# The first expert block's 512 rows prepared in the planned first pass, in the output weights' storage; a bias scaled on ScalarE; new due times

## The chip, the cores and the metric

The kernel runs on one core of a Trainium2 chip. The metric is the device time of one execution in microseconds (us), the median of three runs. A run takes in both layers of the network from the inputs in device memory to the output there; no work is done on the host.

## The reference

The input `x` has 64 graphs of 256 nodes with 256 features, and `adj` is a 0/1 matrix for each graph, stored as int32. Two layers follow one another, each of a graph part and a feed-forward part, and each part adds its result to `x`:

```python
x = x + gat(layernorm(x), adj, W, a)            # softmax over neighbours, 256x256 a graph
x = x + mamba2(layernorm(x), W_in, conv_w, ..., W_out, W_lin, b_lin)   # one chunk of 256, 8 heads of 64
x = x + rgcn(layernorm(x), adj, weight, bias)   # relation ids 1..4; adj holds 0 and 1 here
x = x + moe(layernorm(x), gate_w, gate_b, w1, b1, w2, b2)

# moe: T = 16384 tokens, E = 8 experts, capacity C = ceil(1.25 * T / E) = 2560
idx = argmax(softmax(x @ gate_w + gate_b)); prb = that probability
hmid = relu(buf @ w1[e] + b1[e])                # 256 -> 1024, for the tokens of expert e
y = (hmid @ w2[e] + b2[e]) * prb                # 1024 -> 256, 0 for tokens over the capacity
y = nan_to_num(y, nan=0, posinf=1e4, neginf=-1e4)
```

## The kernel before

The kernel has two passes. **Pass 1** (`first_pass`, line 482) takes the 64 graphs in 32 groups of two. A group is 512 rows, held as four tiles of 128 rows by 256 columns. For each group it runs attention (`attention`), the Mamba block (`scan`, `mix`), the relation part (`relate`), and for every second group the choice of an expert for 1024 tokens (`choose`). `choose` writes for every token a record of four numbers (token number, probability, minus the mean, inverse deviation) into a table `slots` in device memory, at the place that the token has with its expert; this is an indirect DMA on GpSimd, line 1436. The rows themselves go to `x3d` and to the output, line 1361.

Pass 1 isn't run in the order of the code. Every operation is a step (`Plan.step`) with an engine, an assumed duration, what it reads and writes, and a rank. `Plan.record` then issues all steps in an order of its own: of all engines it takes the one whose next step can begin first by the assumed durations, and among steps of one engine that could begin within 0.05 us of each other it takes the one with the smaller rank. The rank is `PACE * g + due`, with `g` the group and `due` an entry of one of two tables: `DUE` has 278 entries, one for each step of a group, and `LATE` has one for each step outside the groups. The order so found is fixed in the program, and each engine then runs its instructions in that order and waits for what each of them needs. Entries 0 and 1 of `DUE` belong to the loads of `x` and `adj` (lines 932 and 935, SyncE's queue), entry 29 to the load of `s2` (line 979), and entries 108 to 111 to the four loads of `spread` (line 1145), from which ScalarE makes the decays (line 1158).

Three **first blocks** (`first_block`, line 1443) are steps of the plan too. Each takes 512 tokens of one expert from the first 28 groups, and serves as filler at the end of pass 1. Their second product is line 1543; each of its four row tiles goes through DVE line 1549, ScalarE line 1551, five DVE instructions (lines 464 to 468, which replace what isn't finite), a DVE addition (line 1557) and an indirect DMA into the output on GpSimd (`sent`, line 477). Their results lie in four buffers `y`, two to a row tile.

The **lead block** is the first block of pass 2. The plan prepares half of it (`lead`, line 840): SyncE fetches its 512 records (line 849), DVE makes indices of them (lines 449 and 450), GpSimd gathers row tiles 0 and 1 from `x3d` into `lead_xg` (line 453), DVE normalises them (line 459), TensorE turns them (line 473), and ScalarE copies the result back over `lead_xg` (line 865).

**Pass 2** (`second_pass`, line 1624) goes through the rest of the tokens, first in whole blocks of 512 and then in quarter blocks of 128, one expert to a block. It is written in program order. Before its first block it issues weights (lines 1672 to 1682), records (line 1662), and gathers of rows: four for block 0 (row tiles 2 and 3 first, then 0 and 1; the raw rows are added to the result at the end), four for block 1, one each for quarter blocks 0 and 1. DVE normalises block 0's row tiles 2 and 3 (`rest`) and then the rows of quarter block 0 (`ahead`). A block (`experts`, line 1714) does this:

- it gathers the rows of the block after the next, and normalises those of the next (`xn`);
- first product: for each of 8 slices of 128 hidden columns two matmuls (line 1732) into a PSUM bank, then ReLU with the first bias on ScalarE (line 1737). Each matmul of the code is two matmul instructions in the profile. Block 0 does this in two halves of 256 rows, with the turning of row tiles 2 and 3 between them (`turned`, lines 1708 and 1711);
- second product: for each row tile 8 matmuls (line 1743), then DVE adds the second bias (line 1748), ScalarE scales by the token's probability (line 1749), and DVE lines 464 to 468 and 1756 and the indirect DMA of line 477 follow;
- after the second row tile of the four, TensorE turns the next block's `xn`, so it stops there until that is ready.

Pass 2's tiles lie where pass 1's were, and wait for these. The tile `wf` (line 507) holds the Mamba block's output weights; it belongs to pass 1 and is read by the matmuls of `mix` alone.

Of the kernel before, what the change touches and what calls it, by code (L numbers as in the profile page):

```python
# [20 lines left out]
P = 128  # L21
# [15 lines left out]
    -6331, -3161, 12771, 6388, -1140, 18799, -8820, -3915, -10864, 15954, -2744, -20439, 7528,  # L37
    -4617, -31541, -17200, 5602, -14762, -8419, -5891, -5603, -1541, -5405, -14791, -3990, 335,
    -20199, -23350, -2083, 2822, 14284, -5071, -6879, 4498, -5782, 6238, -17462, -2816, -33883,
    -20616, -6436, -3048, -8998, -9634, -9504, -22113, -20276, -11261, 1522, -9857, -1653,  # L40
    -15833, -9229, 2924, -22132, -17106, -4387, -35510, -16757, 3569, -2885, 4527, -1412, -8283,
    -15528, -3929, -11779, -11456, -7814, -6057, -12317, -10809, -5133, -8678, 9134, 13953,
    -13794, -23451, -4899, -21639, -22746, -10486, 27012, -17529, -1344, -3836, -5711, -23725,
    -14953, -12879, 3172, -5981, 1591, 15512, -17461, 534, 152, -19929, 1549, 14357, 7195,
    -3419, 29983, -11226, -18919, -14208, -27486, -16133, -19727, -32975, 18680, -3566, -464,
    -8894, -2901, -21861, 7237, -13596, -5780, 12376, 1844, -21884, 4880, -17265, -11181, 7161,
    -21630, 548, 14964, 3358, 3185, 2812, -16559, -8864, 11674, 270, 390, 1481, 9504, 2847,
    2431, 16079, 19662, -3898, 11518, 11847, 506, -17371, 20459, -5279, -20969, 31082, -3253,
    -3595, -970, 18447, 7039, -9745, -11902, -30335, 20548, -30229, -14082, 510, -2197, -25176,
    -18526, -28007, -18182, 10633, -26993, 8938, -10832, -10379, -11184, -15953, -1534, -10200,  # L50
    1179, -1228, -13286, -4161, 9055, 6753, 3161, 9529, -846, 3842, 15756, -9976, -8924, -10517,
    5604, -11994, -14390, -11511, 924, 7080, -3763, -2334, -14368, -21952, -16111, 7133, -3818,
    -13625, -16189, 4478, -3362, -831, -30811, -22197, 9169, -17068, 2289, -22646, -5638,
    -21211, -26355, 7956, -16785, -15433, 4253, -877, 2942, -11894, -10082, 5510, 8259, -10789,
    -3344, 791, -22653, 6991, -2251, -8409, -27482, -21823, -16753, 23439, -12372, -11445, 3310,
    22527, -8655, 2999, 1496, -8271, 10255, -15555, 8288, -35896, -6103, 7904, -13179, -16680,
    5249, -9828, -22280, 12222, -12498, 3441, -987, -8001, -4859, -9609, -5004, -31730, -12922,
    -9059, 5997, -13207, -32473, 21806, -6080, -32608, -5307, -9518,
]
LATE = [  # L60
    -63840, -55520, -59131, -55207, -59848, -61432, -57187, -57822, -56536, -55767, -53926,
    -58374, -60103, -65443, -56691, -53149, -62097, -52465, -58452, -56667, -62610, -54784,
    -65608, -59759, -57377, -56098, -61108, -61167, -57235, -56292, -60029, -60269, -55423,
    -63060, -63414, -59681, -63156, -58243, -64255, -56127, -56108, -57795, -60886, -59513,
    -60777, -59004, -59056, -58806, -59572, -53601, -56191, -58146, -57176, -54847, -56525,
    -55495, -53939, -56747, -58739, -49488, -50233, -60000, -54842, -49112, -48407, -55847,
    -60899, -53242, -54553, -52587, -54497, -52317, -53060, -55827, -53215, -50999, -56633,
    -59606, -52185, -51253, -56189, -53292, -51734, -50652, -43997, -50070, -49882, -48836,
    -53102, -52273, -56157, -60055, -50169, 1013, -1983, -728, -4765, -2369, -6423, -4345,
    -4325, -5261, -3579, -1796, -1630, -5149, -6851, -4608, -3725, -4488, -2136, -8245, -7748,  # L70
    -2950, -8122, 8006, 1788, 4824, -6193, 9606, 8820, 5666, -14159, 1157, -2894, 5812, 508,
    -8873, 9151, 4753, 9855, -1831, 1035, 7140, -2464, 8056, -3647, 371, 308, 3499, 8133, 4587,
    10125, 4843, -72, 332, 712, 3988, -4756, 10239, 636, -6535, -1479, -7990, -162, 6431, 11207,
    6866, 1481, 4338, 5632, 2772, 10504, 2221, -5019, -3263, 6153, 2958, 8184, 463, 3082, 3259,
    -744, 5246, -8874, 224, -2297, -2637, 9968, -5301, 6929, -3923, 12788, 1870, -5152, 7957,
    -1091, 8442, 5255, 977, 9080, 8105, 3506, 9391, 6154, -1644, -1231, 4565, -6856, 7951, 3020,
    10508, -4150, -1421, -3664, -1888, -297, 3392, 868, -3074, 7014, 1260, 2674, 3807, 3088,
    471, -7315, -17345, 4406, 4533, -7940, 10566, 9292, 5735, 7492, 2786, 1767, -4750, -535,
    -1766, 1723, -1381, 846, -1114, 6258, -3949, 4074, -1805, 1084, 6817, -3447, 6810, -3140,
    13076, 2332, 330, 8723, -3860, 7332, 9552, -3530, 12999, 10185, 1587, 11267, 5283, 2368,  # L80
    -565, 6790, -2563, 4983, 3103, 10465, -4403, -3174, -771, -6778, 1016, 4107, -1453, -2923,
    7230, 2679, -268, 4098, -352, 584, -10766, -12316, 7157, 1989, -7855, 10593, 10918, 2783,
    6000, 4603, 6058, -6544, -2195, -2667,
# [235 lines left out]
def gnn_mamba_rgcn_moe(ctx: ExitStack, tc: tile.TileContext, a: dict, out: bass.AP):  # L319
# [109 lines left out]
    lead_xg = const.tile([P, 2, D], F32, name="lead_xg")  # L429
# [40 lines left out]
    def lead_turned(ps):  # L470
        for k in range(2):
            for j in range(2):
                nc.tensor.transpose(
                    ps[:, (2 * k + j) * P : (2 * k + j + 1) * P], lead_xg[:, j, k * P : (k + 1) * P], ident)
# [7 lines left out]
    def first_pass(form, pass1):  # L482
# [24 lines left out]
        wf = wts.tile([P, NCT, DG], F32, name="wf")  # L507
# [332 lines left out]
        def lead(s, listed_, stored):  # L840

            meta_, place_, xg_ = (s.fixed(t) for t in (lead_meta, lead_place, lead_xg))
# [14 lines left out]
            for j in range(2):  # L857
                s.step(POOL, 1.1, lambda j=j: gathered(lead_xg[:, j, :], lead_place[:, 1, j : j + 1], x3d),
                       [place_, *stored], [(xg_, j)], late=2.0, move=0.3)
            for j in range(2):  # L860
                s.step(DVE, 0.33, lambda j=j: normed(lead_xg[:, j, :], lead_xg[:, j, :], lead_meta[:, j, :]),
                       [meta_], [(xg_, j)])
            ps = s.psum()
            s.step(PE, 0.45, lambda: lead_turned(ps()), [xg_], [ps])
            s.step(ACT, 0.48, lambda: nc.scalar.copy(
                lead_xg.rearrange("p j d -> p (j d)"), ps()), [ps], [xg_])
# [757 lines left out]
    def second_pass(form, pass2):  # L1624
# [6 lines left out]
        class Blocks:  # L1631
# [70 lines left out]
            def turned(self, xn, i, js=None):  # L1702

                js, dst = js or range(self.J), self.xnT[i % 2]
                for k in range(2):
                    ps = eps.tile([P, 512], F32, tag="ps", name="ps")
                    for o in range(len(js)):
# [3 lines left out]
                    nc.scalar.copy(  # L1711
                        dst[:, k, js[0] * P : (js[-1] + 1) * P], ps[:, : len(js) * P])

            def experts(self, i, rest=None):

                n = self.J * P
                meta, place, xg = self.meta[i % 3], self.place[i % 3], self.xg[i % 3]
# [157 lines left out]
```

## Time and profile before

| what | value |
|---|---|
| time, median of 3 runs | 2331.28 us (2331.22 to 2331.72) |
| the profiled execution's own time | 2330.76 us |
| its span, first to last instruction | 2328.8 us |
| busy: TensorE, DVE, ScalarE, GpSimd | 2234.8, 1759.9, 1664.4, 912.5 us |
| last instruction of the first blocks' product (line 1543) ends | 1752.3 us |
| last read of `wf` by a matmul begins | 1658.5 us |
| one whole block of pass 2 (from 1797.15 to 1825.58) | 28.43 us |
| first and second product of a whole block | 13.73 and 2 x 6.91 us |

The profiled execution's time is 1.96 us longer than its span, and lies 0.52 us under the median. A row of a timeline gives the start and the duration of an instruction or of several alike, its engine, line and operation, the tiles written and read, and in brackets how long the engine had been idle and which work ended that. PE is TensorE and PEld its loading of weights; POOL is GpSimd; SPq is SyncE's queue of DMA issues. The chain is the work that ended last, followed back step by step; it isn't proof that nothing else was as late.

### The profile page before, as it was taken

The page shows a single profiled execution, that of the slowest core. Times are in us where ns is not written, and L with a number is a line of the kernel's source. Part 1 is how long each engine was busy: PE and PEld are TensorE (multiplying, and loading weights), DVE is VectorE, ACT ScalarE, POOL GpSimd, SP SyncE. Part 2 cuts the span into 40 slices and gives each one's busy share as a digit, 9 for nine tenths or more (in the row PEclk, how much of TensorE's full clock was granted, in tenths as well). Part 3 has the DMA queues.
Part 4 walks back from the last instruction along what each step waited for, and adds up shares of the span by engine and source line. Part 5 has one row for each costly group of instructions (what it writes and reads, how often), then busy time and mean ns, then how long its engine had stood idle before and what let it go on. Part 6 is the DMA issues. An engine that isn't in the chain of part 4 may idle for free.

```text
span 2328.8 us, 34741 instructions
## 1 busy us (share of the span) xinstructions
PE 2234.8 (96%) x11111; PEld 1565.5 (67%) x11111; DVE 1759.9 (76%) x4396; ACT 1664.4 (71%) x3873; POOL 912.5 (39%) x992
## 2 busy tenths in 40 slices
PE   6999999999999999999999999999997999999986
PEld 4676766676776666766776667566676666666665
DVE  3899989999999999999998998799554333333342
ACT  3899989899999899999899988888522223332222
POOL 1233445354443445435354444523543222222221
PEclk7999999999999999999999999999998999999998
DMA  4343445444444445444453554424536333333436
GB/s 141 76 102 99 122 117 126 110 108 108 122 122 121 111 108 118 113 117 126 110 116 101 122 140 107 104 62 122 146 101 229 113 116 116 116 115 117 118 85 192
DMA packets 199928, 274.48 MB, mean 118 GB/s; under 512 B 28472, under 2 KB 165886, under 8 KB 199712
## 3 DMA queue, kind: packets, MB, share of 16 engines
q1 hardware_dynamic: 149968, 211.48, 29.3%
q0 software_dynamic: 46752, 58.65, 13.7%
q8 instruction: 94, 1.54, 0.3%
q10 hardware_dynamic: 2992, 1.81, 0.3%
q14 instruction: 122, 1.00, 0.1%
HBM read 187.43 MB, written 46.04 MB: 100 GB/s over the span
## 4 chain that ended last, share of the span: by engine, by line
PE 58%; ACT 14%; DVE 9%; POOL 6%; issue 6%; DMA 6%; SPq 0%; POOLq 0%; ACTq 0%; DVEq 0%
PE ps L871 27%; PE ps L1743 9%; PE ps L1732 9%; PE ps L1240 4%; POOL slots L1436 3%; ACT dm L1158 3%; PE ps L910 2%; PE ps L1216 2%; PE ps L1244 2%; ACT ev L998 2%; DMA x<-in_x_dram 1%; DMA xg<-x3d,lead_place 1%; ACT dm L1164 1%; DVE y L1098 1%; DVE dm L1232 1%
## 5 line engine op out<-in xcount | busy, mean ns | idle before, releaser
L871 PE MATMUL ps<-xnT,win 128*128 128x512 f32 x1152 | 539.3, 597 | 5.3 <-ACT xnT L915 4.4
L1158 ACT ACTIVATE dm<-spread,cs 128x256 f32<-128x256 f32 (+1 forms) x1024 | 379.1, 452 | 21.8 <-PE ps L1244 20.6
L1098 DVE SCALAR_TENSOR_TENSOR y<-ps,cw,y 128x510 f32<-128x510 f32 (+2 forms) x480 | 353.5, 738 | 34.5 <-ACT y L1091 31.9
L871 PEld LDWEIGHTS ps<-xnT,win 128*128 128x128 f32 x1152 | 206.9, 190 | 178.2 <-issue 157.1
L1743 PE MATMUL ps<-w,hid 128*128 128x256 f32 x1184 | 262.1, 379 | 0.0
L1732 PE MATMUL ps<-xnT,w 128*128 128x512 f32 (+2 forms) x736 | 257.0, 509 | 1.5 <-ACT xnT L1711 1.4
L871 PE MATMUL ps<-wf,gate 128*128 128x265 f32 x1024 | 251.8, 389 | 1.8 <-DVE gate L1254 1.8
L1743 PEld LDWEIGHTS ps<-w,hid 128*128 128x128 f32 x1184 | 223.2, 190 | 36.2 <-issue 7.7
L1232 DVE TENSOR_TENSOR dm<-dm,bc 128x1536 f32<-128x1536 f32 x128 | 224.0, 1750 | 3.0 <-ACT dm L1164 2.4
L871 PEld LDWEIGHTS ps<-wf,gate 128*128 128x128 f32 x1024 | 189.7, 190 | 46.5 <-issue 8.2
L1737 ACT ACTIVATE hid<-ps,b 128x512 f32<-128x512 f32 (+2 forms) x192 | 112.2, 591 | 140.4 <-PE ps L1732 134.5
L1732 PEld LDWEIGHTS ps<-xnT,w 128*128 128x128 f32 x736 | 128.9, 197 | 120.3 <-issue 110.0
L1164 ACT ACTIVATE dm<-dm 128x1536 f32<-128x1536 f32 x128 | 190.0, 1487 | 0.0
L1748 DVE TENSOR_TENSOR yv<-ps,b 128x256 f32<-128x256 f32 x74 | 31.4, 425 | 195.9 <-PE ps L1743 195.7
L1240 PE MATMUL ps<-dm,xdt 128*64 128x256 f32 x1024 | 168.7, 390 | 3.7 <-DVE xdt L1221 2.9
L1436 POOL DMA_INDIRECT slots<-meta,sl x128 | 145.3, 1136 | 59.4 <-issue 31.7
L879 POOL TENSOR_SCALAR ve<-mv 128x4 f32<-128x4 f32 x96 | 37.6, 392 | 322.3 <-DVE mv L892 217.2
L889 DVE BATCH_NORM_STATS2 st<-x 128x6 f32<-128x256 f32 x384 | 151.7, 413 | 8.4 <-DMA x<-in_x_dram 8.2
L871 PE MATMUL ps<-wx,xT 128*128 128x292 f32 x512 | 137.1, 409 | 0.0
L871 PE MATMUL ps<-wrel,hr 128*128 128x265 f32 x512 | 134.4, 392 | 0.8 <-ACT hr L1349 0.8
L871 PE MATMUL ps<-wh,eT 128*128 128x273 f32 x512 | 132.1, 402 | 1.9 <-ACT eT L1016 1.9
L1091 ACT ACTIVATE y<-ps,cb,cw 128x512 f32<-128x512 f32 x160 | 124.1, 776 | 2.1 <-PE ps L871 1.9
(310 smaller groups left out, 4727.8 us busy)
## 6 DMA issues: line engine op xcount, KB each, us to landing
spread<-sumd SPq DMA_DIRECT2D x128, 512.0 KB
w<-in_L_ffn_w_dram SPq DMA_DIRECT2D x50, 1024.0 KB
x<-blin POOLq DMA_DIRECT2D x32, 530.0 KB
x<-brel POOLq DMA_DIRECT2D x32, 530.0 KB
x<-in_x_dram SPq DMA_DIRECT2D x32, 512.0 KB
adji<-in_adj_dram SPq DMA_DIRECT2D x32, 512.0 KB
out_dram<-x SPq DMA_DIRECT2D x32, 512.0 KB
x3d<-x SPq DMA_DIRECT2D x32, 512.0 KB
```

What stands on the lines that cost most here:

```text
L871: nc.tensor.matmul(out_, lhsT=lhsT, rhs=rhs, start=(i == 0), stop=(i == len(pairs) - 1))
L889: s.step(DVE, 0.34, lambda j=j: nc.vector.bn_stats(sb()[:, j, :], src()[:, j, 0:D]), [(src, j)], [(sb, j)])
L1091: s.step(ACT, 0.66, lambda: nc.scalar.activation(y(), ps(), AF.Identity, scale=cw[:, c, 3:4], bias=cb[:, c : c + 1]), [ps, s.fixed(cw), s. ...
L1098: nc.vector.scalar_tensor_tensor(y3[:, :, d:], p3[:, :, : N - d], cw[:, c, k : k + 1], y3[:, :, d:], ALU.mult, ALU.add,)
L1158: nc.scalar.activation(dm()[:, q, bi, o : o + n], spr()[:, q, t1 - n : t1], AF.Relu, bias=cs()[:, 4 * h + j : 4 * h + j + 1], scale=-1.0,)
L1164: s.step(ACT, 1.38, lambda: nc.scalar.activation(dm(), dm(), AF.Exp, scale=-1.0), [], [dm])
L1232: s.step(DVE, 1.67, lambda dm=dm: nc.vector.tensor_mul(dm(), dm(), bc().unsqueeze(1).to_broadcast([P, 2, 2, N + P])), [bc], [dm], port=1)
L1240: nc.tensor.matmul(o, lhsT=xdt()[:, 2 * bi, h * 64 : (h + 1) * 64], rhs=dm()[:, q, bi, 0:N], start=True, stop=False,)
L1436: s.step(POOL, 1.1, lambda j=j: apart("slots", nc.gpsimd.indirect_dma_start(out=slots, out_offset=bass.IndirectOffsetOnAxis(ap=sl()[:, j : ...
L1732: nc.tensor.matmul(ps[:, :m], lhsT=w1[:, k, f * P : (f + 1) * P], rhs=lead_xg[:, k, :] if rest is not None and not o else xnT[:, k, o : o ...
L1737: nc.scalar.activation(hid[:, f, o : o + m], ps[:, :m], AF.Relu, bias=self.b1[i % 2][:, f : f + 1])
L1743: nc.tensor.matmul(ps[:, :D], lhsT=hid[:, f, j * P : (j + 1) * P], rhs=w2[:, f, :], start=(f == 0), stop=(f == NFT - 1),)
```

## The change

Four things are changed.

1. `lead` makes all four row tiles ready. It gathers four instead of two, normalises four, and turns them into two PSUM banks, one for each half of the features, copied by two ScalarE instructions. `lead_xg` is no tile of its own any more: it is a view of `wf`, and `wf` now lies with the constants, so that it lives through pass 2.
2. Block 0 of pass 2 does its first product at once for 512 rows, from the lead's tile. The `rest` normalisation and the turning in the middle are gone; the gathers of raw rows stay, in one loop. Its own turned tile `xnT` for even blocks moves to another pool.
3. In `experts` ScalarE scales the second bias by the probability (`bp`, an instruction ahead of the second product's matmuls in the code), and DVE does product times probability plus `bp` in one instruction. Before, DVE added and ScalarE scaled after it.
4. All entries of `DUE` and `LATE` are new; `LATE` has six more, for the lead's six more steps.

```diff
 DUE = [
-    -6331, -3161, 12771, 6388, -1140, 18799, -8820, -3915, -10864, 15954, -2744, -20439, 7528,
...
-    -20199, -23350, -2083, 2822, 14284, -5071, -6879, 4498, -5782, 6238, -17462, -2816, -33883,
...
-    -3419, 29983, -11226, -18919, -14208, -27486, -16133, -19727, -32975, 18680, -3566, -464,
...
+    -26698, -26684, 16811, 5376, -1385, 22233, -9147, -5334, -6104, 16470, -4131, -12656,
...
+    -5594, 1406, -16327, -16058, -1084, -23798, -1397, -15584, 5401, -4898, -4435, 935, -15679,
...
+    14191, 6307, -9703, 30905, -7622, -19413, -14996, -28968, 116, 19317, 13445, 26060, -32817,
...
-    lead_xg = const.tile([P, 2, D], F32, name="lead_xg")
+    wf = const.tile([P, NCT, D + E + 1], F32, name="wf")
+    lead_xg = wf.rearrange("p c d -> p (c d)")[:, : 4 * D].rearrange("p (j d) -> p j d", j=4)
+    lead_xnT = lead_xg.rearrange("p (k h) d -> p k (h d)", k=2)
...
-    def lead_turned(ps):
-        for k in range(2):
-            for j in range(2):
-                nc.tensor.transpose(
-                    ps[:, (2 * k + j) * P : (2 * k + j + 1) * P], lead_xg[:, j, k * P : (k + 1) * P], ident)
+    def lead_turned(ps, k):
+        for j in range(4):
+            nc.tensor.transpose(ps[:, j * P : (j + 1) * P], lead_xg[:, j, k * P : (k + 1) * P], ident)
...
-        wf = wts.tile([P, NCT, DG], F32, name="wf")
...
-            for j in range(2):
+            for j in range(4):
                 s.step(POOL, 1.1, lambda j=j: gathered(lead_xg[:, j, :], lead_place[:, 1, j : j + 1], x3d),
-                       [place_, *stored], [(xg_, j)], late=2.0, move=0.3)
-            for j in range(2):
+                       [place_, *stored], [(xg_, j)], late=2.0, move=0.5)
+            for j in range(4):
                 s.step(DVE, 0.33, lambda j=j: normed(lead_xg[:, j, :], lead_xg[:, j, :], lead_meta[:, j, :]),
                        [meta_], [(xg_, j)])
-            ps = s.psum()
-            s.step(PE, 0.45, lambda: lead_turned(ps()), [xg_], [ps])
-            s.step(ACT, 0.48, lambda: nc.scalar.copy(
-                lead_xg.rearrange("p j d -> p (j d)"), ps()), [ps], [xg_])
+            both = [s.psum() for _ in range(2)]
+            for k, ps in enumerate(both):
+                s.step(PE, 0.45, lambda k=k, ps=ps: lead_turned(ps(), k), [xg_], [ps])
+            for k, ps in enumerate(both):
+                s.step(ACT, 0.48, lambda k=k, ps=ps: nc.scalar.copy(lead_xnT[:, k, :], ps()), [ps], [xg_])
...
-                for o, m in ((0, n),) if rest is None else ((0, n // 2), (n // 2, n // 2)):
-                    if o:
-                        self.turned(rest, i, (2, 3))
-                    for f in range(NFT):
...
+                turned = lead_xnT if i == 0 and self.kind == 0 else xnT
+                for f in range(NFT):
+                    ps = eps.tile([P, 512], F32, tag="ps", name="ps")
+                    for k in range(2):
+                        nc.tensor.matmul(
+                            ps[:, :n], lhsT=w1[:, k, f * P : (f + 1) * P], rhs=turned[:, k, :],
+                            start=(k == 0), stop=(k == 1),
                         )
+                    nc.scalar.activation(
+                        hid[:, f, :], ps[:, :n], AF.Relu, bias=self.b1[i % 2][:, f : f + 1]
+                    )
                 for j in range(self.J):
+                    bp = es.tile([P, D], F32, tag="bp", name="bp")
+                    nc.scalar.activation(bp, self.b2[i % 2], AF.Copy, scale=meta[:, j, 1:2])
...
                     yv = es.tile([P, D], F32, tag="yv", name="yv")
-                    nc.vector.tensor_add(yv, ps[:, :D], self.b2[i % 2])
-                    nc.scalar.activation(yv, yv, AF.Copy, scale=meta[:, j, 1:2])
+                    nc.vector.scalar_tensor_tensor(
+                        yv, ps[:, :D], meta[:, j, 1:2], bp, ALU.mult, ALU.add)
...
-        for name in ("w1", "b1", "b2", "xnT", "xg"):
+        for name in ("w1", "b1", "b2", "xg"):
             wholes.room(ea, name, 0)
...
-        wholes.room(et, "xnT", 1)
+        for i in range(2):
+            wholes.room(et, "xnT", i)
...
-        wholes.gather(0, None, (2, 3))
-        rest = wholes.norm(0, (2, 3), tag="rest", bufs=1, pool=ea)
-        wholes.gather(0, None, (0, 1))
+        wholes.gather(0, None)
```

## The prediction

> **What bounds the kernel now.** I read the page first, then the busy time by stage, then the waits of TensorE, then the chain and the timeline around the change of passes. The page:
>
> ```profile
> span 2328.8 us, 34741 instructions
> ...
> PE 2234.8 (96%) x11111; PEld 1565.5 (67%) x11111; DVE 1759.9 (76%) x4396; ACT 1664.4 (71%) x3873; POOL 912.5 (39%) x992
> ```
>
> TensorE is the bound, but the 94 us in which it is idle are not spread evenly. By stage, from 100 to 1740 us it is busy for 1610.52 of 1640 us, so all stalls of pass 1's main part are 29.5 us together. The change of passes is different (busy time of an engine in each stretch, then TensorE's granted clock, DMA share and GB/s):
>
> ```profile
> core 0: us, PE busy (x) PEld busy (x) DVE busy (x) ACT busy (x) POOL busy (x), PEclk, DMA share, GB/s
> 1752.13:1761.45 9.32, 7.34 (x33) 5.81 (x31) 6.20 (x20) 3.08 (x8) 1.97 (x2) 1.00 0.56 183
> 1761.45:1772.74 11.29, 1.35 (x4) 0.69 (x4) 1.20 (x5) 1.34 (x4) 8.68 (x11) 0.63 0.85 291
> 1772.74:1782.30 9.56, 9.56 (x32) 7.96 (x33) 1.31 (x6) 3.69 (x8) 3.57 (x8) 0.73 1.06 361
> 1782.30:1796.99 14.69, 14.69 (x73) 12.99 (x72) 7.95 (x23) 2.96 (x6) 5.49 (x6) 1.00 0.44 151
> 1796.99:1825.58 28.59, 28.59 (x106) 19.23 (x105) 11.30 (x34) 8.49 (x14) 7.86 (x8) 1.00 0.37 116
> ```
>
> The first row is the first half of block 0's first product. Then comes a hole of 11.3 us. The next row is the second half: the same 32 instructions that need 6.86 us (half of a whole block's 13.73) take 9.56 us, at a clock of 0.73. So block 0 takes 1796.99 - 1752.13 = 44.9 us where the next takes 28.4: 16.4 us are lost here. The timeline tells why (gather, DVE, TensorE rows in order of time):
>
> ```profile
> 1743.54 0.99 POOL L453 DMA_INDIRECT lead_xg<-x3d,lead_place  x1 [3.35 <-DVE lead_place L450]
> 1744.84 0.98 POOL L453 DMA_INDIRECT lead_xg<-x3d,lead_place  x1 [0.30 <-issue]
> 1747.96 0.41 DVE L459 TENSOR_SCALAR lead_xg<-lead_xg,lead_meta 128x256 f32<-128x256 f32 x1 [0.29 <-DMA lead_xg<-x3d,lead_place]
> ...
> 1756.79 0.29 DVE L465 TENSOR_SCALAR y<-y 128x256 f32<-128x256 f32 x1 [2.27 <-DMA out_dram<-y,hide]
> ...
> 1761.55 0.97 POOL L477 DMA_INDIRECT out_dram<-y,hide  x1 [1.43 <-DVE ones L1819]
> 1762.83 0.98 POOL L453 DMA_INDIRECT xg<-x3d,lead_place  x1 [0.30 <-issue]
> ...
> 1769.77 0.41 DVE L459 TENSOR_SCALAR xn<-xg,lead_meta 128x256 f32<-128x256 f32 x1 [7.88 <-DMA xg<-x3d,lead_place]
> 1770.33 0.45 PE L1708 MATMUL ps<-ident,xn 128*128 128x128 f32 x1 [8.88 <-DVE xn L459]
> ...
> 1774.12 1.02 POOL L453 DMA_INDIRECT xg<-x3d,place  x1 [0.16 <-issue]
> ...
> 1780.66 0.41 DVE L459 TENSOR_SCALAR xn<-xg,meta 128x256 f32<-128x256 f32 x1 [8.91 <-DMA xg<-x3d,place]
> ...
> 1781.56 1.42 DVE L459 TENSOR_SCALAR xn<-xg,meta 128x256 f32<-128x256 f32 x4
> ```
>
> Read it as one queue. GpSimd's last send of a first block (1761.55) stands ahead of pass 2's ten gathers, one every 1.29 us. The first of these lands after 6.9 us, and only then can row tiles 2 and 3 be normalised and turned. The row at 1780.66 matters as much: it is `ahead`, quarter block 0's normalisation, which waits for a gather issued at 1774.12, and block 1's four `xn` (1781.56) stand behind it on DVE.
>
> **Part 1 and 2: the lead.** TensorE's work stays equal (64 instructions of 256 columns become 32 of 512, 13.73 us either way); two copies of 256 columns (0.80 us) leave pass 2, and one of 512 more (0.59 us) enters the plan. Two gathers are added. They issue at 1746.1 and 1747.4 (1.29 us apart, after 1744.84). GpSimd idles 3.8 us before its next send at 1749.60, so 2.6 us fit. The two first landed 3.7 to 4.4 us after issue (1743.54 to 1747.96, 1744.84 to 1748.58); those nearest in time later took 6.9 and 7.2 us. So the last row lands between 1751.1 and 1754.6; plus 0.41 us normalising, 1.04 us for eight transposes (row at 1789.21), 0.59 us for a copy, and the hops, the first product begins between 1753.3 and 1756.7. I take 1754.5: 2.4 us later than now, because the filler (line 1543, to 1752.3) is used up. DVE's two more normalisations (0.8 us) lie beside its 2.27 us wait at 1754.5. `wf` adds no wait: its last reader begins at 1658.5, 85 us earlier. Nor do the weights: the DMA rate falls to 3 GB/s at 1758, so block 0's have landed by then, and the second product needs its own at 1768. With `wf` and `xnT` elsewhere, pass 2's tiles lie over other tiles of pass 1. SyncE's loads for block 1 already wait 10.8 us for the first blocks' end (line 1679, up to 1761.30) and are used after 1790. I take nothing for it; 1.5 us more of waiting would be covered as well.
>
> Then block 0 needs no rows until its end: first product to 1768.2, row tiles 0 and 1 of the second to 1775.1. **What is late next** is block 1's `xn`: in program order TensorE turns them there. Nothing in parts 1 to 3 moves the sends, the ten gathers or `ahead`, so they are still ready at 1783.0. TensorE stalls 7.9 us instead of 8.9. Its transposes end at 1783.3, and row tiles 2 and 3 follow, at a fallen clock again: 6.91 us plus the 2.7 us that the same kind of hole cost in the third row above. Block 1 begins at 1792.9 instead of 1797.0: **4.1 us gained of 16.4**. Ends: if the stall were gone, block 1 would begin at 1754.5 + 28.43 = 1782.9, gain 14.1; if the sends or `ahead` come 4 us later (the lead's two more gathers and normalisations standing ahead of them, 2.6 + 0.8 us, plus a hop), nothing is gained.
>
> The Trainium skill, "TensorE: Matmul & The Clock Gate", Part 1, says that TensorE falls to half its clock after an idle window of about 3.4 us and returns after as long a busy one. That would cost half of 3.4, an estimate of 1.7 us, where the row shows 2.7; by it the gain would be 5.1 us. The rule speaks against the change as far as it leaves a hole behind: shortened by 1 us, it would cost as much as before.
>
> **Part 3: the bias.** In whole blocks TensorE never stops (28.59 of 28.59 us), and nothing waits for DVE; ScalarE has as many instructions as before (one of 0.51 us a row tile), beside 8.49 of 28.59 us. There it is worth nothing, covered by TensorE; without that cover it would be the hop. The hop: DVE's addition begins at 2251.95, line 464 behind it at 2253.01, 1.06 us. Two DVE instructions of this size that follow directly are 0.46 us apart (lines 467 and 468), and the joined one may be 0.05 longer (0.485 for line 1312, read from PSUM, against 0.427 for line 1358). So 0.55 us a hop. It is on the path twice: TensorE waits for DVE's queue between the whole and the quarter blocks (5.8 us), and the last row tile's send ends the kernel. **1.1 us**, between 0 (if another engine's branch is the later) and 1.2.
>
> **Part 4: the tables.** Every entry is new, so the order of all steps of pass 1 is. The trace of before can't show it. The bounds: better by at most what TensorE idles from 100 to 1740 us, 29.5 us; worse by as much, if it idles twice as long; no row excludes either. The nearest rows are waits with a table entry behind them. The loads of x and adj go to the front of their ties, and TensorE waited 5.9 us in all, in 5 pieces, for x from memory. I take half of it, **3 us**. The loads of `spread` go back; ScalarE waited for them for only 0.9 us in all.
>
> **Sum:** 4.1 + 1.1 + 3 = 8.2 us off 2330.76 gives 2322.6 for an execution like the profiled one; the median lies 0.5 higher, 2323.1, so 2323.
>
> **The rivals.** A difference under 0.2%, 4.7 us, can't be told from no change here.
>
> - *A, the forecast: half the hole moves to block 1's turning.* 2323; with the tables between 0 and 6 us, 2320 to 2326. For it: `ahead` and its gather are untouched. Chance 0.42.
> - *B, the hole closes.* If the new order ends the first blocks' sends some 8 us earlier, the gathers begin earlier, block 1's rows are there, and the gain is 14.1: 2331.3 - 14.1 - 1.1 - 3 = 2313, and 2309 with 4 us more from the tables. For it: the last sends wait for line 465, which waits 2.27 us for a buffer `y`, a matter of order. Against: DMA runs at 0.85 and 1.06 of its share where the gathers land. Chance 0.18.
> - *C, the gain is eaten:* the change doesn't do what it says. The two more gathers and normalisations delay the sends by 4 us, and block 1 begins where it did. 1.1 us from the bias and nothing or 1 us from the tables: 2329 to 2330. Chance 0.22.
> - *D, slower: the new ranks starve ScalarE of `spread`.* A load of `x` chosen ahead of `spread` takes 3.9 to 5.5 us by the chain, and decays, DVE's products and TensorE's heads (line 1240) wait behind it. With 0.5 us reaching TensorE in each of 32 groups it costs 16 us: 2331.3 + 16 - 5.2 = 2342. It decides from (5.2 + 4.7) / 32 = 0.31 us a group. For it: DVE and ScalarE are over 90% busy from 100 to 1300 us, so a late decay isn't made up. Against: the 0.9 us above. Chance 0.18.
>
> **How the numbers follow.** Faster by over 0.2%: A and B, 0.60. Within: C, 0.22. Slower: D, 0.18. A to C reach from 2309 to 2330; B beyond 2309 (tables better still) and D beyond 2340 hold together less than 2 in 10. So 2309 to 2340, across both signs because the tables' bounds are wide.
>
> **What would show it.** The first product of block 0 as 32 instructions of 512 columns in about 13.7 us from 1754 or so, with no stop inside (parts 1 and 2). A TensorE wait of about 8 us for `xn` ahead of the transposes after row tile 1, and a clock under 1 behind it (A); no such wait (B); a block 1 that begins at 1797 less whatever pass 1 gained (C). Line 464 0.5 us after the joined instruction. TensorE's busy time from 100 us to the last group, against 29.5 us idle, and its waits for x (part 4); ScalarE's waits for `spread` (D). I'm wrong in kind if pass 1 moves by over 10 us either way, since the tables then outweigh all that the trace could tell.

## The result, and the profile after

The kernel after takes 2339.8 us (median of 6 runs, 2334.83 to 2343.47) beside 2331.04 us for the kernel before (6 runs, 2327.34 to 2331.72): ratio 1.0035, 95% interval 1.0024 to 1.0046. It is **slower**, by 0.35%, where faster was forecast. The profiled execution of after took 2334.83 us, the lowest of its six runs; 4 us longer than before's, where the medians differ by 8.8. The page of after:

```profile
span 2333.0 us, 34723 instructions
...
PE 2234.0 (96%) x11079; PEld 1561.5 (67%) x11079; DVE 1756.9 (75%) x4396; ACT 1664.6 (71%) x3864; POOL 918.5 (39%) x994
```

TensorE does the same work in a longer span. The change of passes, by stage (in the columns of the prediction's table: first product of block 0, row tiles 0 and 1 of its second, the stall, the rest of block 0, block 1):

```profile
core 0: us, PE busy (x) PEld busy (x) DVE busy (x) ACT busy (x) POOL busy (x), PEclk, DMA share, GB/s
1765.04:1778.90 13.86, 13.86 (x34) 6.22 (x33) 4.55 (x16) 6.46 (x12) 8.07 (x11) 1.00 0.74 236
1778.90:1785.80 6.90, 6.89 (x32) 5.73 (x31) 0.00 (x0) 0.69 (x1) 4.97 (x9) 1.00 0.99 328
1785.80:1790.40 4.60, 0.00 (x0) 0.00 (x0) 1.10 (x5) 0.00 (x0) 0.18 (x1) 0.74 1.08 345
1790.40:1800.60 10.20, 10.18 (x41) 8.63 (x42) 8.41 (x24) 2.59 (x5) 6.26 (x7) 0.78 0.51 182
1800.60:1829.00 28.40, 28.40 (x105) 19.09 (x104) 11.55 (x34) 8.39 (x14) 7.83 (x9) 1.00 0.36 117
```

The lead does what it says: the first product runs without a stop, and what is left of the hole has moved in front of block 1's transposes, with a low clock behind it. Block 0 takes 35.6 us (1765.0 to 1800.6) instead of 44.9. But it begins 12.9 us later than in before (1752.1), and block 1 to the end takes 532.4 us beside 531.8. So 12.9 - 9.3 + 0.6 = 4.2 us, the difference of the spans: **the loss lies in pass 1.** There TensorE is busy for 1602.05 us from 100 to 1740 us; before it was 1610.52. Its waits in that window, first before (engine, what waited, for whom: us in total, times, longest):

```profile
PE ps L910 <- DMA x<-in_x_dram: 5.9, 5, 2.0
PE ps L1009 <- ACT ev L998: 3.7, 13, 0.6
```

and after:

```profile
PE ps L1009 <- ACT ev L998: 11.4, 22, 0.9
PE ps L910 <- DMA x<-in_x_dram: 5.3, 6, 1.6
PE ps L1216 <- DVE xh L1108: 3.2, 1, 3.2
```

The waits for `x`, which part 4 counted on, hardly move. A new one leads: line 1009 is the turn of the attention weights `ev` on TensorE, and waits for ScalarE's exponentials (line 998). It comes twice in each pair of groups, 0.88 and 0.16 us at 11 places from 298 to 1302 us, where before had one of some 0.25 us from 403 us on. A pair now takes 99.7 to 99.9 us where it took 99.0 to 99.2 (from one `lg` copy of line 1368 on ScalarE to the next but one); every kernel here has some longer pairs, around 400, 700 to 800 and 1200 us. The ten pairs from the fourth copy (at about 354 us) to the 24th take 1003.5 us, in before 996.0: 7.5 us.

### The profile page after: what moved, and what is told of

Its sections match the earlier page's. It is cut to its first block, busy times and chain, and to the rows that moved or that the text cites. A ratio compares the mean times of both kernels' runs of the same rounds, so it can differ in the third digit from the quotient of the medians.

```text
span 2333.0 us, 34723 instructions
## 1 busy us (share of the span) xinstructions
PE 2234.0 (96%) x11079; PEld 1561.5 (67%) x11079; DVE 1756.9 (75%) x4396; ACT 1664.6 (71%) x3864; POOL 918.5 (39%) x994
## 4 chain that ended last, share of the span: by engine, by line
PE 39%; issue 21%; ACT 13%; POOL 11%; DVE 9%; DMA 5%; SPq 0%; POOLq 0%; ACTq 0%; DVEq 0%
PE ps L871 26%; PE ps L1240 4%; POOL slots L1436 3%; POOL out_dram L477 3%; POOL xg L455 3%; ACT dm L1158 3%; PE ps L910 2%; DVE y L1098 2%; PE ps L1244 2%; ACT dm L1164 1%; ACT xh L1256 1%; ACT xn L925 1%; DMA x<-in_x_dram 1%; PE ps L1543 1%; DMA xg<-x3d,lead_place 1%
## 5 line engine op out<-in xcount | busy, mean ns | idle before, releaser
L1730 PE MATMUL ps<-xnT,w 128*128 128x512 f32 (+1 forms) x704 | 247.3, 511 | 1.4 <-ACT xnT L1711 1.4
L871 PEld LDWEIGHTS ps<-wf,gate 128*128 128x128 f32 x1024 | 190.6, 190 | 44.9 <-issue 11.7
L1734 ACT ACTIVATE hid<-ps,b 128x512 f32<-128x512 f32 (+1 forms) x184 | 110.6, 603 | 133.0 <-PE ps L1730 130.0
L1730 PEld LDWEIGHTS ps<-xnT,w 128*128 128x128 f32 x704 | 121.3, 195 | 118.1 <-issue 110.8
L1436 POOL DMA_INDIRECT slots<-meta,sl x128 | 153.8, 1202 | 50.6 <-issue 30.9
L1747 DVE SCALAR_TENSOR_TENSOR yv<-ps,meta,bp 128x256 f32<-128x256 f32 x50 | 24.2, 484 | 161.7 <-PE ps L1742 150.9
L1711 ACT COPY xnT<-ps 128x512 f32<-128x512 f32 (+1 forms) x48 | 21.5, 496 | 151.8 <-PE ps L1708 151.8
L871 PE MATMUL ps<-wh,eT 128*128 128x273 f32 x512 | 127.0, 396 | 0.5 <-ACT eT L1016 0.5
```

Source lines behind the costliest of these rows:

```text
L871: nc.tensor.matmul(out_, lhsT=lhsT, rhs=rhs, start=(i == 0), stop=(i == len(pairs) - 1))
L1436: s.step(POOL, 1.1, lambda j=j: apart("slots", nc.gpsimd.indirect_dma_start(out=slots, out_offset=bass.IndirectOffsetOnAxis(ap=sl()[:, j : ...
L1730: nc.tensor.matmul(ps[:, :n], lhsT=w1[:, k, f * P : (f + 1) * P], rhs=turned[:, k, :], start=(k == 0), stop=(k == 1),)
L1734: nc.scalar.activation(hid[:, f, :], ps[:, :n], AF.Relu, bias=self.b1[i % 2][:, f : f + 1])
```

## The experiments

Medians are of 4 to 11 runs; a ratio is against the kernel before, measured beside it on the same chip, with its 95% interval. The median of before lay between 2330.07 and 2333.23. In the views an edited kernel's lines are shifted; the names of the tiles tell which instruction it is.

| run | edit | us | ratio |
|---|---|---|---|
| e1_old_tables | after, old tables | 2328.14 | 0.9986 (0.9977 to 0.9995) |
| e2_new_tables | before, new tables | 2338.26 | 1.0026 (1.0016 to 1.0036) |
| e3_bias | before, new bias | 2335.08 | 1.0013 (1.0004 to 1.0022) |
| e4_again | after, unedited | 2340.16 | 1.0036 (1.0022 to 1.005) |
| e5_lead | before, lead | 2328.02 | 0.9985 (0.9976 to 0.9994) |
| e6_due | before, new `DUE` | 2347.65 | 1.0073 (1.006 to 1.0087) |
| e7_late | before, new `LATE` | 2333.0 | 1.0011 (1.0002 to 1.002) |
| e8_turns | after, turns later | 2338.19 | 1.0035 (1.0022 to 1.0049) |
| e9_root | after, GpSimd's order of before | 2387.88 | 1.0238 (1.0224 to 1.0252) |
| e10_sends | after, sends last | 2317.7 | 0.9937 (0.9924 to 0.9951) |
| e13_root | after, root alone earlier | 2352.7 | 1.0094 (1.008 to 1.0107) |
| e14_adds | after, additions alone earlier | 2397.24 | 1.0291 (1.0277 to 1.0305) |
| e11_rows | e5, block 1's `xn` first on DVE | 2323.38 | 0.9958 (0.9945 to 0.9972) |
| e12_both | e11, sends last | 2313.72 | 0.9915 (0.9902 to 0.9929) |
| e15_new | e10, block 1's rows first | 2311.02 | 0.9915 (0.9902 to 0.9929) |
| e16_old | e5, sends last, rows first | 2309.06 | 0.9907 (0.9892 to 0.9922) |
| e17_bias | e16, new bias | 2309.81 | 0.9901 (0.9883 to 0.9919) |
| e18_again | e16, unedited | 2306.57 | 0.9899 (0.9882 to 0.9915) |

**The parts, one by one.** The tables:

```diff
 DUE = [
-    -26698, -26684, 16811, 5376, -1385, 22233, -9147, -5334, -6104, 16470, -4131, -12656,
...
+    -6331, -3161, 12771, 6388, -1140, 18799, -8820, -3915, -10864, 15954, -2744, -20439, 7528,
...
```

> The changed kernel with the old due times (the lead's six added steps take the entries of their neighbours), so pass 1 is issued as in the kernel before and only the lead and the bias differ. Theory T (the new order of pass 1 costs 8 us or more, the lead gains 4.3, the bias 0.6): 2331.0 - 4.9 = 2326 us, block 1 of pass 2 begins at about 1793 us. Rival S (the moved storage or the two added gathers cost the time, and the tables nothing): 2335 to 2340 us, as the changed kernel.

> The kernel before with the new due times alone (the entries of the six added steps dropped). Theory T: the last product of the first blocks ends 8 us later than before, the hole of 11 us stays, so 2331 + 8 = 2339 us, and with what the changed kernel's median lies above its profiled run up to 2344. Rival S: within 1 us of 2331.

> The kernel before with the second bias scaled on ScalarE alone. By the prediction's step 1.1 us less, 2330; by the trace of the changed kernel (block 1's start to the end of the span 531.8 us in the place of 532.4) 0.6 us less. A rival, that ScalarE's added work ahead of the ReLUs costs pass 2 something: 2331 to 2333.

> The changed kernel once more, unedited, for a second profile and its spread. Its six times ran from 2334.8 to 2343.5 us, those of the kernel before from 2327.3 to 2331.7. If the spread comes from pass 1 (an order with no slack that some executions run through with more waits), the profile shows other lengths of some pairs of groups than the first one, and the same 532 us from block 1 to the end. If it comes from pass 2, the pairs are alike and the 532 us differ. Median 2338 to 2342.

e4 repeats the result. The tables are the loss: with the old ones the change gains 3 us, with the new ones alone before loses 6, and e2's pairs take as long as after's (99.7 to 100.0 us). The two together lie some 5 us above the sum of the two alone; in after's profile there is a wait of 2.8 us of the lead's turning for the last row, with filler standing behind it, which can be a part of that:

```profile
1757.83 0.27 PE L474 MATMUL ps<-ident,wf 128*128 128x128 f32 x1
1760.86 1.75 PE L474 MATMUL ps<-ident,wf 128*128 128x128 f32 x7 [2.76 <-DVE wf L461]
1762.41 2.75 PE L1543 MATMUL ps<-xh,x 128*128 128x256 f32 x8
```

The lead alone is e1 without the bias (the edit against e1); the two runs behind it have one table each:

```diff
-                    bp = es.tile([P, D], F32, tag="bp", name="bp")
-                    nc.scalar.activation(bp, self.b2[i % 2], AF.Copy, scale=meta[:, j, 1:2])
...
-                    nc.vector.scalar_tensor_tensor(
-                        yv, ps[:, :D], meta[:, j, 1:2], bp, ALU.mult, ALU.add)
+                    nc.vector.tensor_add(yv, ps[:, :D], self.b2[i % 2])
+                    nc.scalar.activation(yv, yv, AF.Copy, scale=meta[:, j, 1:2])
```

> The kernel before with the lead block's changes alone (parts 1 and 2; old tables, old bias). The theory that the lead is worth 4.2 us and the bias nothing: block 1 of pass 2 begins near 1793, and the median is 4 us under the kernel before, about 2327 (ratio 0.998). The rival that the bias costs the 3 us by which its own run lay above the kernel before: then the lead is worth 6 to 7 us, and this run is near 2324 (0.997). The rival that the lead is worth no more than the 3 us of the run with old tables: 2328, and the bias is worth nothing either way.

> The kernel before with the new table of the groups' due times alone. The theory that the loss of pass 1 comes from the turn of the attention weights, which the groups' table puts one projection too early: all of it is here, 6 to 8 us, so 2337 to 2339 (ratio 1.0027 to 1.0033), and a pair of groups takes 99.7 to 100 us where before takes 99.1. The rival that the loss comes from what stands outside the groups (first blocks, choice of blocks, lead) in another order: within 2 us of the kernel before.

> The kernel before with the new table of the steps outside the groups alone (the lead's six further entries left out). By the theory that the groups' table costs the time this is within 2 us of the kernel before, and a pair of groups takes 99.1 us. The rival that the first blocks at the end of pass 1 come in a worse order: 3 to 8 us longer, with the last first-block product ending after 1756 instead of at 1752.

The lead alone is worth what it is worth with the bias (e1). TensorE's rows of e5 at the change of passes:

```profile
1753.29 14.00 PE L1730 MATMUL ps<-wf,w 128*128 128x512 f32 x32 [0.46 <-ACT wf L866]
1767.13 7.07 PE L1740 MATMUL ps<-w,hid 128*128 128x256 f32 x32
1781.84 2.31 PE L1708 MATMUL ps<-ident,xn 128*128 128x128 f32 x8 [7.63 <-DVE xn L461]
1783.94 8.88 PE L1740 MATMUL ps<-w,hid 128*128 128x256 f32 x32
1792.66 7.89 PE L1730 MATMUL ps<-xnT,w 128*128 128x512 f32 x18
```

Block 1 begins at 1792.7 (1797.0 in before). `DUE` carries the loss of the pairs; without its own `LATE` it costs 9 us more, at the end of pass 1 (the first blocks' product ends at 1779.8, in e2 at 1761.1). `LATE` alone costs some 2 us (by the interval 0.5 to 4.7) and leaves the pairs at 99.0 to 99.2 us. The new `DUE` changes the order less than thought. In the traces of before and e6, in the pair from about 1053 to 1153 us, 17 of TensorE's 537 instructions, 38 of DVE's 222, 28 of ScalarE's 219 and 3 of GpSimd's 49 stand elsewhere.

**The turn.** One of these places is on TensorE, in the rows around the turn, after and before:

```profile
1096.64 1.96 PE L871 MATMUL ps<-wf,gate 128*128 128x265 f32 x8
1098.43 1.88 PE L871 MATMUL ps<-xnT,win 128*128 128x512 f32 x4
1101.19 0.33 PE L1009 MATMUL ps<-ident,ev 128*128 128x128 f32 x1 [0.88 <-ACT ev L998]
```

```profile
1092.90 1.96 PE L871 MATMUL ps<-wf,gate 128*128 128x265 f32 x8
1094.69 3.60 PE L871 MATMUL ps<-xnT,win 128*128 128x512 f32 x8
1098.12 0.60 PE L1009 MATMUL ps<-ident,ev 128*128 128x128 f32 x4
```

One projection (x4) stands ahead of the turn instead of two (x8). So the next run gives the turns their old place (the order of TensorE's steps, in short):

```diff
-turn, projection, turn, projection
+projection, turn, projection, turn
```

> The kernel after with one edit to the recorded order: at the 13 places where TensorE's order has turn of attention weights, projection, turn, projection (one place in each pair of groups), each turn is issued after the projection that followed it, as the kernel before has it; nothing else moves on any engine. The theory that the wait of the turn for ScalarE's exponentials costs the 0.6 us a pair: 13 x 0.6 = 8 us go, the median is near 2332 (2330 to 2334), TensorE's waits of that line fall from 16.7 to about 9 us, and a pair takes 99.1 us. The rival that pass 1 is bound by something else in the new order, so that the wait only moves to another line: 2337 to 2341, with the same period of the pairs and as much idle time under another line.

The theory fell. The pairs keep 99.7 us, and the wait sits one instruction group later, at the copy `eT` of the turned weights:

```profile
PE ps L907 <- ACT eT L1052: 14.2, 12, 1.3
PE ps L946 <- DMA x<-in_x_dram: 5.5, 6, 1.5
```

What is late is what ScalarE waits for. The chain of waits of after, from GpSimd to ScalarE (start, us, what; in the view of its longest pieces):

```profile
1088.32 1.39 POOL slots L1436
1089.80 0.97 issue
1090.77 0.97 POOL slots L1436
1092.05 0.97 POOL slots L1436
1093.02 1.08 POOL r2r L1309
1094.13 0.56 DVE x L1312 x2
1095.79 0.63 DVE y L1098
1096.75 0.65 DVE y L1098
1097.51 0.63 ACT xh L1104
1098.15 0.60 ACT ev L998 x2
1099.15 1.37 ACT dm L1164
```

Read from the bottom: ScalarE's exponentials stand in its queue behind a convolution, that waits for DVE, whose queue stands behind `r2r`, the inverse root of the Mamba norm, and this stands on GpSimd behind the sends of `choose` into `slots`. Nobody waits for a send (from 300 to 1400 us no engine does, in before or after). In before the chain passes the sends too, and leaves them by line 983, the additions `hm` that the exponentials need.

**GpSimd's sends.** Once in a pair there are 8 sends, a root and two additions. The edits, given in short, change only their order, at 11 pairs:

```diff
-send x7, root, add, send, add
+send x3, root, send x5, add x2
```

> The kernel after with one edit to the recorded order, on GpSimd alone: at the 11 places, one in each pair of groups, where its order has 7 sends to the slots (line 1436), the inverse root (line 1309), an addition (line 983), the eighth send and the second addition, it gets the order of the kernel before: 3 sends, the root, 5 sends, both additions. The theory that in the new order the inverse root stands 4 sends too late, and that DVE, the convolution behind it, ScalarE's queue and so the turn of the attention weights wait for it: the period of a pair falls from 99.7 to 99.1 us, 11 x 0.65 = 7 us go, 2332 to 2333. The rival that the additions of line 983, which stay behind all eight sends, hold the pair back as much: less than 2 us, 2338 to 2340.

```diff
-send x7, root, add, send, add
+send x3, root, add x2, send x5
```

> The kernel after, with GpSimd's order at the same 11 places: 3 sends, the inverse root, both additions, and the other 5 sends behind them, into the 6 to 7 us that GpSimd idles there. Now neither the root nor the additions stand behind more than 3 sends. The theory that GpSimd's 15 us of sends in a row set the period of a pair, in before and in after: it falls to 98.3 to 99.0 us, 11 x 0.7 to 1.4 = 8 to 15 us go, 2325 to 2332. The rival that ScalarE and DVE, both over 90% busy there, hold the period whatever GpSimd does: 2336 to 2340, and 99.5 us or more a pair.

e10 gains 22 us on after, and e9 loses 48; neither run's theories had that. In e10 GpSimd's stretch is (line 1469 is the send, 1340 the root, 1012 the additions)

```profile
1067.50 1.30 POOL L1469 DMA_INDIRECT slots<-meta,sl  x1 [0.73 <-DVE sl L1466]
...
1071.83 1.07 POOL L1340 TENSOR_TENSOR r2r<-r,mhalf 128x4 f32<-128x4 f32 x1
1075.17 2.29 POOL L1012 TENSOR_TENSOR hm<-hide,s 128x512 f32<-128x512 bf16 x2 [2.27 <-DMA s<-s2d]
1077.63 1.04 POOL L1469 DMA_INDIRECT slots<-meta,sl  x1 [0.17 <-issue]
...
1082.79 0.97 POOL L1469 DMA_INDIRECT slots<-meta,sl  x1 [0.30 <-issue]
1087.56 0.23 POOL L908 TENSOR_SCALAR ve<-mv 128x4 f32<-128x4 f32 x1 [3.81 <-DVE mv L921]
```

The additions now wait for their input, `s`, and not for sends, and 3.8 us of idle time are left behind the last send. A pair takes 97.8 us, less than in before, and the turn's wait is down to 1.3 us in all. To tell the root from the additions:

```diff
-send x7, root, add, send, add
+send x3, root, send x4, add, send, add
```

> The kernel after with GpSimd's order edited at the 11 places: the inverse root (line 1309) alone goes four sends earlier (3 sends, root, 4 sends, addition, send, addition); the additions of line 983 keep their place behind all that. If the root alone sets the period of a pair in the new order, as its chain of waits reads, it falls from 99.7 to 98 us as in the run with both moved: 2318 to 2324. If the additions set it, nothing is gained: 2337 to 2341.

```diff
-send x7, root, add, send, add
+send x3, add x2, send x4, root, send
```

> The kernel after with the opposite edit: both additions of line 983 go ahead of the fourth send, the root stays behind the seventh and comes by 2.3 us later than before the edit (3 sends, both additions, 4 sends, root, send). If the additions alone set the period, 2318 to 2324. If the root sets it, each pair becomes 2.3 us longer: 2340 + 11 x 2.3 = 2365. If both lie within a microsecond of each other, as two inputs of the same queues of DVE and ScalarE, both this run and the one with the root alone lie above 2334.

Ends of the root and of the first addition, in us from the start of the first send, with the time of a pair (without the longer ones named above):

| kernel | root | first addition | pair |
|---|---|---|---|
| before (old order elsewhere) | 5.4 | 13.6 | 99.1 |
| after | 11.7 | 12.8 | 99.7 |
| e10_sends | 5.4 | 8.6 to 11.6 | 97.8 |
| e13_root | 5.4 | 13.15 | 100 to 101.9 |
| e9_root | 5.4 | 14.4 | 103.3 to 104.9 |
| e14_adds | 15.4 to 17.4 | 8.2 to 10.2 | 103.5 to 105.0 |

Both were late: the third case of e14's expectation. Moving the root alone left the additions late; moving the additions alone made the root later, and then TensorE waits for DVE line 1312 itself (its line 1352 there):

```profile
PE ps L907 <- DVE x L1352: 51.3, 11, 5.8
```

With e9, e13 and after the pair grows with the end of the addition. Why 0.33 us more of it costs 1 us or more a pair in e13 is not settled. Part of e9's and e14's loss is a lower clock (mean 0.971 and 0.973, in after 0.985) that came with stalls of 3.7 and 5.8 us. That the order of before bears an addition at 13.6 us fits its turn: TensorE reaches it 19.1 us after the first send (1098.12 - 1079.03), in after at 17.9 (1101.19 - 0.88 - 1082.40). The new order asks 1.2 us earlier and gets the additions 0.8 us earlier. Which of the moved steps makes it ask earlier stays open: putting TensorE's turns back (e8) changed nothing, and GpSimd's order back (e9) cost 48 us.

That the tables' loss comes by way of this queue is shown by what is left of it when the sends are out of the way. e15 has the new tables and e16 the old, both with the sends last and block 1's rows first: 2311.02 and 2309.06 us, 2.0 us apart, and pairs of 97.8 and of 97.5 to 98.3 us. With the sends in their places after and e5, which differ in the same way, lie 0.5% apart, some 12 us.

**The rest of the hole.** The stall before block 1's transposes (the code also gathers block 1's rows first):

```diff
+        xn_1 = wholes.norm(1, tag="xn1", bufs=1, pool=ea)
         ahead = quarters.norm(0, tag="ahead", bufs=1)
```

> The kernel before with the lead's changes, and in pass 2 block 1's rows first: gathered ahead of quarter block 0's, block 0's raw rows and quarter block 1's, and normalised by DVE ahead of quarter block 0's. The theory of the prediction's part 2, that after the lead is done TensorE waits only for block 1's rows, which stand behind block 0's raw rows and behind the normalisation of quarter block 0: the 7.6 us stall in front of block 1's transposes goes, with the slow clock behind it, and block 1 begins at 1753.3 + 28.4 = 1782 instead of 1792.7: 10 us less than the run with the lead alone, 2318. The rival that the rows land no earlier, since the weights' 1 MB loads fill the DMA queues then (300 to 430 GB/s): block 1 begins after 1789, 2324 to 2328.

> The kernel of the run with block 1's rows first, with GpSimd's order changed in pass 1 as well: at the 10 places where the old order has 3 sends, root, 5 sends, both additions, the 5 sends go behind the additions. By the theory that GpSimd's sends set the period of a pair in the old order too: 0.5 to 0.9 us a pair, 5 to 9 us less than the run with the rows alone, 2309 to 2313 if that is 2318. By the rival that ScalarE and DVE hold the period: within 2 us of that run.

In e11 and e12 only DVE's order changed: pass 2 isn't held to the order of its code, and on GpSimd block 0's raw rows stayed first. `xn` came when its rows did, one gather after another, at 1778.6 to 1782.2, and block 0 took 34.9 us: between the two theories. e12 shows the sends' price in the old order, 2323.4 - 2313.7 = 10 us. Of the 11 us by which block 0 was too long in e5, 6.5 were left in e11. The next runs hold GpSimd to the written order:

```diff
+        with tc.manual_schedule(engines={mybir.EngineType.Pool}):
+            wholes.gather(1, nc.gpsimd)
+            quarters.gather(0, nc.gpsimd)
+            wholes.gather(0, None)
+            quarters.gather(1, nc.gpsimd)
```

> The kernel after with the sends behind the additions (the run at 2317.7 us) and with pass 2's gathers in an order that is now kept as written: block 1's four, quarter block 0's, block 0's raw rows, quarter block 1's; block 1's rows are normalised ahead of quarter block 0's. By the theory of part 2 block 0 then has no stall: 28.4 to 29.5 us instead of 34.5, so 5 to 6 us less, 2312. By the rival that the gathers are slow because of the weights' loads, whatever their order, less than 2 us: 2316 to 2318.

> The same two edits on the kernel before with the lead's changes alone (old tables, old bias), which so far stood at 2313.7 us with the sends moved and DVE's order changed, but with the gathers still in the old order. By the theory of part 2 block 0 falls from 34.1 to 28.4 to 29.5 us, and the median to 2308 or 2309. By the rival of the weights' loads 2312 to 2314.

> The fastest kernel so far (2309 us: old tables, lead, sends behind the additions, block 1's rows first) with the bias change added. The prediction's part 3: 1.1 us less than the same kernel without it in the same comparison. The theory from the profiles: the hop of 0.45 us is won at the change from whole to quarter blocks, given back in the next block, and the last send is not what ends the program, so it is worth nothing: within 1 us. The rival from the run with the bias alone (3 us over the kernel before): 2 to 4 us more.

> The same fastest kernel without the bias change, as the yardstick of the run with it: 2309 us again, 2308 to 2311.

The hole is closed in e17 and e18. TensorE's rows of e18:

```profile
1741.65 14.00 PE L1768 MATMUL ps<-wf,w 128*128 128x512 f32 x32 [0.46 <-ACT wf L895]
1755.49 7.07 PE L1778 MATMUL ps<-w,hid 128*128 128x256 f32 x32
1762.40 1.04 PE L1743 MATMUL ps<-ident,xn 128*128 128x128 f32 x8
1763.27 7.07 PE L1778 MATMUL ps<-w,hid 128*128 128x256 f32 x32
1770.18 5.31 PE L1768 MATMUL ps<-xnT,w 128*128 128x512 f32 x12
```

Block 0 takes 28.5 us, as any other, at the full clock. In the profiles of e15 and e16 it took 30.5 and 30.7 us: e15 has a stop of 1.1 us ahead of block 1, for ScalarE's `bp`, and e16 four of some 0.3 us in the last row tiles. With 2309.06 and 2306.57 us this kernel, without the new tables and without the bias, is 1% faster than before, the fastest of all. With the bias the median is 3.2 us higher (e17 beside e18), as it was in e3; but with four runs each, and ratios of 0.9901 and 0.9899 whose intervals nearly coincide, no difference can be told. The 3 us of e3 are not shown to be the bias's either: its profile is 7.4 us longer than before's, and 4.6 us of these lie ahead of block 0, where the edit changes nothing. No comparison here shows the bias as a gain.

## Why the prediction was wrong

**Part 1 and 2, right.** Block 1 was to begin at 1792.9 with the lead: 1792.7 and 1792.8 in e5 and e1, so close because two errors offset each other. The first product was to begin at 1754.5 (1753.3), block 1's `xn` to be ready at 1783.0 (1781.37 + 1.40), the stall to be 7.9 us (7.63). The transposes ended 0.6 us later than forecast, and row tiles 2 and 3 of the second product took 0.9 us less (8.7 instead of 9.6). Gain predicted 4.1, measured 4.3 at the start of block 1 and 3.1 in the medians. A part is given back behind it: from block 1 to the end e5 takes 534.0 us beside 531.8, and the profiles with the lead 532.2 to 534.3 where those without it have 530.5 to 532.2. Why is not settled. The slow clock cost (2.31 - 1.04) + (8.88 - 7.07) = 3.1 us against the rows at full clock, where the prediction's row gave 2.7. In after block 0 is 9.3 us shorter and begins 12.9 us later.

The Trainium skill, "TensorE: Matmul & The Clock Gate", Part 1, whose idle window of about 3.4 us led to an estimate of 1.7 us for the same cost, differs from the 3.1 us measured here, and the measurement decides.

**Part 3, mis-sized:** 1.1 us taken, nothing that can be told found. The hop itself is as predicted: in e1 the joined instruction takes 0.48 us, and the next on DVE starts 0.52 us after it. At the change to the quarter blocks TensorE waits 5.35 to 5.46 us (e1, e3, e17, after) instead of 5.80. But the quarter block behind it takes 9.7 to 10.2 us in these runs instead of 9.70, and the span ends 21.8 to 21.9 us after the last product on TensorE in before, in after and in e3 alike. "The last row tile's send ends the kernel" was the wrong step: the end didn't move by the hop. The step "covered by TensorE" has an exception too, in block 0, where `bp` stands ahead of the ReLUs in ScalarE's queue. In e1 it comes late, and TensorE stops 2.9 us for `hid`:

```profile
1768.10 1.70 ACT L1739 ACTIVATE bp<-b,lead_meta 128x256 f32<-128x256 f32 x4 [7.90 <-issue]
1769.71 4.71 ACT L1734 ACTIVATE hid<-ps,b 128x512 f32<-128x512 f32 x8
1770.42 8.98 PE L1742 MATMUL ps<-w,hid 128*128 128x256 f32 x32 [2.94 <-ACT hid L1734]
```

There it costs nothing, since block 1's rows come later still: block 0 takes 39.4 us in e1 as in e5.

**Part 4, the step that failed:** "I take half of it", a gain of 3 us from the tables. TensorE's waits for `x` fell by 0.6 us, and in all its idle time in pass 1 grew by 8.5 us (29.5 to 37.95 us from 100 to 1740 us), 7.7 us of it at the turn; in the medians the new tables alone cost 6 to 7 us (e2). Six entries out of 278 were weighed, the loads of `x`, `adj` and `spread`, and one wait was given a price because it could be seen; the estimate was put on the side of a gain though the bounds were even. "So the order of all steps of pass 1 is" was wrong as well: in a pair 3 to 17% of an engine's instructions moved, and what they brought closer together was a turn and its inputs, which had hardly any slack: in before too the turn waits, some 0.25 us a pair. The page had a sign of it that was not read: in before the chain passes GpSimd's sends (3% of the span), in both pairs between 900 and 1100 us, and goes from there through the queues of DVE and ScalarE.

**The rivals.** D had the sign and by luck nearly the time (2342), and not the cause: ScalarE's waits for `spread` went from 0.9 us to none. What came late to ScalarE were the convolution behind the root and the attention's input behind the additions, both by way of GpSimd's queue, which the prediction never priced. A holds for pass 2 taken alone, as e5 shows. B's hole closed only when the gathers' order was changed (e18). C's delay of sends and gathers by the lead itself didn't occur: in e5 the last send is at 1761.75, in before at 1761.55.

## What to carry to other kernels

A table of ranks for a list scheduler is an edit to every queue at once: compare the recorded orders engine by engine and follow each moved step along the chain before giving the table a price, and without that hold a loss as likely as a gain. When moving a waiting instruction only moves the wait, go up the chain to work that nobody waits for in a queue that somebody does: five sends put behind the root and two additions were worth 22 us, on an engine that is 39% busy. When a hole is half filled, ask what stands first in the queues for what it waits for next: block 0 fell from 44.9 to 39.4 us by the lead (e5), and to 28.5 us by gathers and normalisations in another order (e18).

## What the runs showed of the hardware that was not expected

- Of eight indirect sends in a row the longest took 1.65 us in before, 2.15 in after and 2.5 in e9 and e13, in every pair the same; the plain ones take 0.97. It is the seventh in before, the fifth in after and the fourth in e9 and e13, so another order of the same work makes another send the long one. Why is open.
- Four stalls of 0.3 to 1.1 us within 4 us brought nearly as low a clock as one of 7.6 us: in e11 it is 0.74 from 1778.7 to 1783.8 us and 0.77 in the 9 us behind, in e5 0.71 in the stall and 0.73 behind it.
- A kernel's runs spread by up to 10 us (before: 2325.98 to 2336.16 in 21 runs), so that with the 4 to 11 runs of a kernel here a part of 1 us can't be told as a difference of two kernels, and a single profile shows one run of these.
